# Layer-norm statistics of a Swin block: channels folded to 64 a half, one group of products in place of two, and the deviations spread by way of memory

## The chip, the cores and the metric

The kernel runs on one NeuronCore of a Trainium2 chip. The metric is the device time of one execution in microseconds (us). Each kernel ran several times; a "fast" run is one within 1.5% of the fastest of its kernel. PE is TensorE, PEld its weight loads, DVE is VectorE, ACT is ScalarE, POOL is GpSimd, SP the engine that issues most transfers.

## The reference

The input is 16 images of 192 channels, 56 x 56, fp32. The first layer is a Swin block with shifted 7 x 7 windows, the second a dynamic 3 x 3 depthwise convolution. What matters here are the two layer norms over the 192 channels of every token:

```python
def _ln(x, g, b, eps=1e-05):
    mu = x.mean(-1, keepdims=True)
    var = ((x - mu) ** 2).mean(-1, keepdims=True)
    return (x - mu) / jnp.sqrt(var + eps) * g + b

h = _ln(transpose(x), norm1_g, norm1_b)      # before the attention
...                                          # windows, qkv, softmax, projection
x1 = shortcut + transpose(h)
y = _ln(transpose(x1), norm2_g, norm2_b)     # before the MLP
y = gelu(y @ fc1_w + fc1_b) @ fc2_w + fc2_b
return x1 + transpose(y)                     # the convolution follows
```

## The kernel before

An image is cut into 4 steps. A step holds two halves h of 392 tokens (`T`). Channels lie on partitions: `v0[128, 2, T]` has the first 128 channels of both halves, `v1[128, T]` the other 64, half 0 on partitions 0 to 63 and half 1 on 64 to 127. 64 steps are pipelined: while the MLP of step i-2 and the attention of step i run, "side 0" prepares norm 1 of step i+2 or i+3 (names `1_...`) and "side 1" prepares norm 2 of step i-1 or i (names `2_...`).

The channel sums come from products with a constant `sel` of 1/192. The 192 channels are first folded to 128:

```python
def norm_squares(key, i, side, engine, adder=None, tags=None):
    ...
    if engine is nc.scalar:
        for h in range(2) if tags else (slice(0, 2),):
            nc.scalar.activation(s0[:, h], v0[:, h], AF.Square)
        nc.scalar.activation(s1, v1, AF.Square)
    else:
        engine.tensor_tensor(s0, v0, v0, ALU.mult)
        engine.tensor_tensor(s1, v1, v1, ALU.mult)
    ...     # on GpSimd, for each half: s0[p, h] += s1[p]

def norm_sums(key, i, side):
    ...     # xs: copies of v0, and on GpSimd for each half: xs[p, h] = v0[p, h] + v1[p]

def norm_stats(keys, steps):
    ...
    for k in (0, 2) if folded else range(3):
        for side in keys:
            for h in range(2):
                p = (side if k < 2 else 1 - side) * 64 + h * 32
                dst = stats[side][p : p + 32, :T]
                if k == 0 and folded:
                    mm(dst, sel[:, 0], xss[keys[side]][:, h], True, True)
                ...
                else:
                    mm(dst, sel[:, 0], sqs[keys[side]][:, h], True, True)

def norm_spread(keys, d, queues=(nc.sync,), tags=("dv1", "sq01"), order=(1, 0)):
    ...     # for each side, half and block of 32 partitions: one copy of 32 rows
            queues[...].dma_start(v[p : p + 32, h], d[at : at + 32])
```

The MLP's first product is where the statistics sit. `take(f)` gives product f its PSUM banks A, B, C, D, A, B; `gelu(f)` on ScalarE empties them; `between()` puts the statistics into C:

```python
for f in range(3):
    take(f); long(dsts[f], wf1, cols(f), y0, True)
for f in range(3):
    short(dsts[f], wf1, cols(f), y1, False); gelu(f)
after()                     # ScalarE and VectorE: pieces of the convolution
for f in range(3, NFC):
    take(f); short(dsts[f], wf1, cols(f), y1, True)
between()                   # norm_stats into bank C, norm_vars
for f in range(3, NFC):
    long(dsts[f], wf1, cols(f), y0, False); gelu(f)
```

So the short products 4 and 5 wait for the gelus 0 and 1, and the statistics wait for gelu 2.

Names in the profile: `ph` is this first product of the MLP and `hid` what the gelus make of it, `st` the statistics, `dev` and `dv` the deviations (at last their reciprocals) before and after the spread, `yn` the normalised input of the MLP and `win` that of the attention, `sc` the attention scores and `e` their sums with the biases, `pq`, `pk` and `pe` the queries and keys, `y` a piece of the convolution.

## Time and profile before

| before | value |
|---|---|
| time, median | 3108.94 us (3107.64 to 3109.79, 4 runs) |
| loop step, start of ph to start of ph | mostly 47.0 to 47.1 us, every fourth 47.5 |
| statistics in a loop step | 1.45 to 1.55 us, in two steps 1.59 and 1.62 |
| granted TensorE clock | 0.994 |

In each group of instructions the first number is busy time, the second the mean duration of one, and behind the bar stands the engine's idle time just before, with what ended it. Idle time of an engine that is not the bottleneck costs nothing. The prediction reads the page; one view that it did not use matters later, the waits of the weight loads between 200 and 2950 us (columns: who waited for whom, us in total, times, longest):

```profile
PEld sc L92 <- ACT hid L630: 32.6, 58, 0.8
PEld st L92 <- ACT hid L630: 32.4, 58, 0.6
PEld ph L92 <- ACT hid L630: 13.3, 47, 0.4
```

Weight loads run ahead of the products, so such a wait need not cost TensorE anything: its products waited 0.2 us in the same stretch. But it names what the products are close to waiting for: the gelus (`hid`), for ph, st and the scores.

### The profile page before, as it was taken

Reading aid. Unit: us, or ns where it says so; the run is one execution under the profiler, and the core shown is the slowest. Engines: PE = TensorE matmul, PEld = TensorE weight load, DVE = VectorE, ACT = ScalarE, POOL = GpSimd, SP = SyncE. Lnnn points to the kernel's source line nnn. Section 1 sums busy time; section 2 is a strip of 40 time slices with the busy share of each in tenths; the row PEclk is TensorE's granted clock in tenths of the full one; section 3 lists DMA queues with packets and bytes.
Section 4 is the critical chain, followed back from the end, with each engine's and each line's share of the span. In section 5 each row is a group of like instructions: output and inputs, shape, how many; then the busy total and the mean of one; then the engine's idle time right before and its main releaser. Section 6 shows DMA issues by size and latency. Waiting matters only on the chain.

```text
span 3105.7 us, 64444 instructions
## 1 busy us (share of the span) xinstructions
PE 3073.1 (99%) x25670; PEld 1927.8 (62%) x25670; DVE 2118.6 (68%) x3893; ACT 1880.4 (61%) x2989; POOL 1245.4 (40%) x1165
## 2 busy tenths in 40 slices
PE   8999999999999999999999999999999999999998
PEld 5566666666666666666666666666666666666654
DVE  6665676776776766866866767667667668667664
ACT  4665665665655655656656656556556556566553
POOL 7534434334334334344344343343343343443321
PEclk8999999999999999999999999999999999999999
DMA  4102121121211112121121211212111121211101
GB/s 114 30 19 63 41 70 37 45 67 43 68 43 51 52 51 66 35 71 41 43 69 41 70 38 43 69 43 67 45 45 56 48 71 35 65 46 43 35 30 55
DMA packets 98376, 160.09 MB, mean 52 GB/s; under 512 B 25284, under 2 KB 80556, under 8 KB 96156
## 3 DMA queue, kind: packets, MB, share of 16 engines
q1 hardware_dynamic: 95698, 153.10, 17.7%
q8 instruction: 203, 3.33, 0.5%
q0 software_dynamic: 1872, 2.07, 0.4%
q10 hardware_dynamic: 506, 0.79, 0.1%
q14 instruction: 97, 0.79, 0.1%
HBM read 41.26 MB, written 38.54 MB: 26 GB/s over the span
## 4 chain that ended last, share of the span: by engine, by line
PE 96%; DVE 2%; DMA 1%; ACT 0%; issue 0%; POOL 0%; POOLq 0%; DVEq 0%; ACTq 0%
PE ph L92 25%; PE pf L92 24%; PE pv L92 8%; PE pp L92 8%; PE po L92 6%; PE pq L92 5%; PE pt L540 5%; PE sc L92 4%; PE pk L92 4%; PE pe L92 4%; PE st L92 3%; PE pc L92 0%; DMA rel_r<-in_L_conv_rel_bias_dram 0%; DVE vbd L483 0%; DVE e L518 0%
## 5 line engine op out<-in xcount | busy, mean ns | idle before, releaser
L92 PE MATMUL pf<-hid,wf 128*128 128x392 f32 (+1 forms) x3072 | 802.9, 494 | 3.5 <-ACT hid L630 2.0
L92 PE MATMUL ph<-yn,wf 128*128 128x392 f32 (+1 forms) x3072 | 799.1, 497 | 0.3 <-DVE x L616 0.3
L527 POOL TENSOR_TENSOR prob<-e,tot 113x588 f32<-113x588 f32 x256 | 297.7, 1174 | 1126.3 <-DVE tot L526 1126.1
L92 PEld LDWEIGHTS ph<-yn,wf 128*128 128x128 f32 (+1 forms) x3072 | 426.3, 188 | 344.8 <-issue 77.6
L92 PEld LDWEIGHTS pf<-hid,wf 128*128 128x128 f32 (+1 forms) x3072 | 386.9, 164 | 303.2 <-issue 119.7
L483 ACT COPY vbd<-pv 49x192 f32<-49x192 f32 x512 | 160.1, 313 | 682.8 <-DVE vbd L483 678.3
L676 DVE SCALAR_TENSOR_TENSOR x<-pf,cols,x 128x784 f32<-128x784 f32 (+1 forms) x128 | 106.1, 829 | 530.3 <-PE pf L92 494.8
L630 ACT ACTIVATE hid<-ph,f1b 128x784 f32<-128x784 f32 x384 | 336.8, 913 | 102.3 <-PE ph L92 100.8
L266 POOL TENSOR_TENSOR sq<-sq,sq 64x392 f32<-64x392 f32 x252 | 260.8, 1035 | 261.6 <-ACT sq L257 248.2
L280 POOL TENSOR_TENSOR xs<-x,x 64x392 f32<-64x392 f32 x246 | 249.0, 1012 | 231.8 <-DVE x L616 222.5
L740 DVE SCALAR_TENSOR_TENSOR y<-x,wt,y 128x770 f32<-128x770 f32 x282 | 320.1, 1145 | 16.2 <-ACT y L732 8.8
L92 PEld LDWEIGHTS pv<-wqkv,win 64*128 64x128 f32 (+1 forms) x2048 | 255.5, 189 | 30.8 <-issue 0.7
L92 PE MATMUL pv<-wqkv,win 64*128 64x192 f32 (+1 forms) x2048 | 272.3, 326 | 0.0
L518 DVE TENSOR_TENSOR e<-e,top 113x588 f32<-113x588 f32 x256 | 264.0, 1031 | 8.9
L92 PE MATMUL pp<-o,wp 128*128 128x392 f32 (+2 forms) x896 | 251.4, 514 | 0.0
L546 ACT COPY prt<-pt 128x678 f32<-128x678 f32 x256 | 179.2, 727 | 117.1 <-PE pt L540 115.6
L245 ACT ACT_TABLE_LOAD x192 | 246.3, 1283 | 5.2 <-issue 1.8
L511 DVE TENSOR_TENSOR e<-sc,bias_t 113x588 f32<-113x588 f32 x256 | 179.5, 763 | 96.9 <-PE sc L92 96.8
L521 ACT ACTIVATE e<-e 113x588 f32<-113x588 f32 x256 | 176.8, 691 | 110.4 <-DVE e L518 110.4
L540 PEld LDWEIGHTS pt<-ident,prob 113*128 113x128 f32 x1536 | 165.5, 141 | 65.4 <-issue 36.1
L92 PE MATMUL po<-prt,vbd 128*64 128x49 f32 x6144 | 197.1, 224 | 0.4 <-ACT prt L546 0.4
L92 PEld LDWEIGHTS po<-prt,vbd 128*64 128x64 f32 x6144 | 188.9, 138 | 9.7 <-ACT prt L546 0.6
(169 smaller groups left out, 4079.9 us busy)
## 6 DMA issues: line engine op xcount, KB each, us to landing
dv<-dev SPq DMA_DIRECT2D x1004, 49.0 KB, 2.0
xs<-x SPq DMA_DIRECT2D x246, 98.0 KB, 2.2
x<-in_x_dram SPq DMA_DIRECT2D x15, 1484.0 KB, 6.7
out_dram<-y SPq DMA_DIRECT2D x48, 392.0 KB, 2.4
out_dram<-y SPq DMA_DIRECT2D x48, 196.0 KB, 3.2
x<-in_x_dram SPq DMA_DIRECT2D x16, 392.0 KB, 4.5
x<-in_x_dram SPq DMA_DIRECT2D x15, 350.0 KB, 5.5
out_dram<-y SPq DMA_DIRECT2D x16, 308.0 KB, 2.2
```

What stands on the lines that cost most here:

```text
L92: nc.tensor.matmul(dst, lhs, rhs, start=start, stop=stop, skip_group_check=True)
L245: nc.scalar.activation(junk, eps_t[0:1], func)
L266: adder.tensor_tensor(s0[p, h], s0[p, h], s1[p], ALU.add)
L280: nc.gpsimd.tensor_tensor(s0[p, h], v0[p, h], v1[p], ALU.add)
L511: nc.vector.tensor_tensor(e, sc[:PW, :, : HEADS * N], rel, ALU.add)
L518: nc.vector.tensor_tensor(ehs[wp], ehs[wp], t.broadcast_to([PW, 2 * HEADS, N]), ALU.subtract)
L521: nc.scalar.activation(es[wp], es[wp], AF.Exp)
L527: nc.gpsimd.tensor_tensor(prob[wp][:PW, :, 0:N], ehs[wp], t.broadcast_to([PW, 2 * HEADS, N]), ALU.mult)
L540: nc.tensor.transpose(pt[:, a, g * PW : (g + 1) * PW], prob[wp][:PW, h : h + 2, :].rearrange("p h k -> p (h k)"), ident[:PW, :PW],)
L546: nc.scalar.copy(prt, pt[:, :, : 3 * PW])
L630: nc.scalar.activation(hid[:, f], phs[f][:, :, :T], AF.Gelu, bias=f1b[:, f : f + 1])
L740: nc.vector.scalar_tensor_tensor(dst, src, wt[:, kc, t : t + 1], dst, ALU.mult, ALU.add)
```

## The change

The intent is to halve TensorE's time for the statistics. x and the squares of a half are folded further, from 128 channels to 64, which leaves room for both halves on 128 partitions: half 0 on partitions 0 to 63, half 1 on 64 to 127. One product then gives both halves, and both sides' x and squares fill the four column groups at once. The price is a third addition for x and a second kind of square for the crossed-over copy. The reciprocal deviations then go to memory in one transfer and come back by one broadcast read for each side, 3 transfers in place of 16. At the start, the first spread is made by two products and the first normalisation goes ahead of the biases.

```diff
+    def norm_folded(key, i, side):
+        ...
+        own = [(slice(h * 64, h * 64 + 64), h) for h in range(2)]
+        def copies():
+            nc.sync.dma_start(xs[0:64, 1], v0[64:128, 0])
+            nc.sync.dma_start(xs[64:128, 1], v0[0:64, 1])
+        def sums():
+            for p, h in own:
+                nc.gpsimd.tensor_tensor(xs[p, 0], v0[p, h], v1[p], ALU.add)
+            nc.gpsimd.tensor_tensor(xs[:, 0], xs[:, 0], xs[:, 1], ALU.add)
+        def squares(engine):
+            ...                       # s1 = v1 * v1 on GpSimd (2_) or ScalarE (1_)
+            return [
+                lambda: [nc.scalar.activation(s0[p, 0], v0[p, h], AF.Square) for p, h in own],
+                lambda: nc.scalar.activation(s0[:, 1], xs[:, 1], AF.Square),
+            ]
+        def fold():
+            nc.gpsimd.tensor_tensor(s0[:, 0], s0[:, 0], s1, ALU.add)
+            nc.gpsimd.tensor_tensor(s0[:, 0], s0[:, 0], s0[:, 1], ALU.add)
...
     def norm_stats(keys, steps, st):
+            if folded:
+                streams[side] = [(2, x_)]
+                streams[side + 2] = [(2, q_)]
...
+            mm(st[at * 32 : at * 32 + 32, 0, :T], sel[:, which], src, k == 0, k == n - 1)
...
     def norm_vars(keys, st, tag="dev"):        # was: one Square and one subtract for each side
+        nc.scalar.activation(part, st[lo:hi, 0, :T], AF.Square)
+        nc.vector.tensor_tensor(part, st[64 + lo : 64 + hi, 0, :T], part, ALU.subtract)
...
     def norm_spread(keys, part, tags=("dv1", "sq01"), order=(1, 0)):
+        nc.sync.dma_start(rows, part[::16])
...
+            nc.sync.dma_start(
+                v,
+                rows[at : at + 2].rearrange("(o h) t -> o h t", o=1).broadcast_to([128, 2, T]),
+            )
...                                             # end of a loop step
-            norm_sums(f"2_{i}", i, 1)
+            copies, sums_, squares, fold = norm_folded(f"2_{i}", i, 1)
+            copies()
+            rest = squares(nc.gpsimd)
+            sums_()
...
-            norm_squares(f"2_{i}", i, 1, nc.scalar)
+            for f in rest:
+                f()
+            fold()
```

More of the change, by code (lines that the diff above doesn't have):

```diff
@@ L79, in tile_swin_then_dynamic_conv @@
     psum = ctx.enter_context(tc.tile_pool(name="psum", bufs=1, space=bass.MemoryType.PSUM))
+    dram = ctx.enter_context(tc.tile_pool(name="dram", bufs=2, space=bass.MemoryType.DRAM))
     def banks(name, k):
         return psum.tile([128, 2, 512], F32, tag=f"pair{k}", name=name)
-    singles = [None]
-    def bank(k):
-        return singles[0][:, k]
     def mm(dst, lhs, rhs, start, stop):
@@ L239, in flat_of, with norm_squares @@
         return v0.rearrange("p h r c -> p h (r c)"), v1.rearrange("p r c -> p (r c)")
-    sqs, xss, stats = {}, {}, {}
+    sqs, xss = {}, {}
     def table(func):
         nc.scalar.activation(junk, eps_t[0:1], func)
-    def norm_squares(key, i, side, engine, adder=None, tags=None):
+    def norm_squares(key, i, side, engine, tags=None):
         v0, v1 = flat_of(i)
@@ L260, in norm_squares @@
             engine.tensor_tensor(s1, v1, v1, ALU.mult)
-        sqs[key] = s0
-        def add(adder):
-            for h in range(2):
-                p = slice(h * 64, h * 64 + 64)
-                adder.tensor_tensor(s0[p, h], s0[p, h], s1[p], ALU.add)
-        if adder is False:
-            return add
-        add(adder or nc.gpsimd)
-    def norm_sums(key, i, side):
-        v0, v1 = flat_of(i)
-        s0 = one.tile([128, 2, T], F32, tag=("xs", "o")[side], name=f"xs_{key}")
-        nc.sync.dma_start(s0[64:128, 0], v0[64:128, 0])
-        nc.sync.dma_start(s0[0:64, 1], v0[0:64, 1])
-        for h in range(2):
-            p = slice(h * 64, h * 64 + 64)
-            nc.gpsimd.tensor_tensor(s0[p, h], v0[p, h], v1[p], ALU.add)
-        xss[key] = s0
@@ L283, in norm_stats @@
-    def norm_stats(keys, steps):
-        for side in keys:
-            stats[side] = bank(side)
-        folded = all(k in xss for k in keys.values())
-        for k in (0, 2) if folded else range(3):
-            for side in keys:
-                v0, v1 = flat_of(steps[side])
-                for h in range(2):
-                    p = (side if k < 2 else 1 - side) * 64 + h * 32
-                    dst = stats[side][p : p + 32, :T]
-                    if k == 0 and folded:
-                        mm(dst, sel[:, 0], xss[keys[side]][:, h], True, True)
-                    elif k == 0:
-                        mm(dst, sel[:, 0], v0[:, h], True, False)
-                    elif k == 1:
-                        mm(dst, sel[:, 1 + h], v1, False, True)
-                    else:
-                        mm(dst, sel[:, 0], sqs[keys[side]][:, h], True, True)
-        for side in keys:
-            sqs.pop(keys[side])
-            xss.pop(keys[side], None)
@@ L307, in norm_vars @@
-    def norm_vars(keys, tag="dev"):
-        sides = sorted(keys)
-        d = one.tile([128, T], F32, tag=tag, name=f"dev_{keys[sides[0]]}")
-        mean = {s: slice(s * 64, s * 64 + 64) for s in sides}
-        var = {s: slice(64 - s * 64, 128 - s * 64) for s in sides}
-        for s in sides:
-            nc.scalar.activation(d[var[s]], stats[s][mean[s], :T], AF.Square)
-        for s in sides:
-            nc.vector.tensor_tensor(d[var[s]], stats[s][var[s], :T], d[var[s]], ALU.subtract)
-        stats.clear()
-        return d[0:128] if len(sides) == 2 else d[var[sides[0]]], d
+        sqs[key] = s0, s1
@@ new lines, in norm_folded @@
+    def norm_folded(key, i, side):
+        v0, v1 = flat_of(i)
+        xs = one.tile([128, 2, T], F32, tag=("xs", "o")[side], name=f"xs_{key}")
+        s0 = one.tile([128, 2, T], F32, tag=f"sq0{side}", name=f"sq0_{key}")
+        s1 = one.tile([128, T], F32, tag=f"sq1{side}", name=f"sq1_{key}")
+        own = [(slice(h * 64, h * 64 + 64), h) for h in range(2)]
[7 more added lines that the diff above has]
+        def squares(engine):
+            if engine is nc.gpsimd:
+                nc.gpsimd.tensor_tensor(s1, v1, v1, ALU.mult)
+            else:
+                nc.scalar.activation(s1, v1, AF.Square)
+            return [
[5 more added lines that the diff above has]
+            nc.gpsimd.tensor_tensor(s0[:, 0], s0[:, 0], s0[:, 1], ALU.add)
+        xss[key] = xs[:, 0], s0[:, 0]
+        return copies, sums, squares, fold
@@ new lines, in norm_stats @@
+    def norm_stats(keys, steps, st):
+        folded = all(k in xss for k in keys.values())
+        streams = {}
+        for side, key in keys.items():
+            if folded:
+                x_, q_ = xss.pop(key)
+                streams[side] = [(2, x_)]
+                streams[side + 2] = [(2, q_)]
+            else:
+                v0, v1 = flat_of(steps[side])
+                s0, s1 = sqs.pop(key)
+                streams[side] = [(0, v0[:, 0]), (1, v0[:, 1]), (2, v1)]
+                streams[side + 2] = [(0, s0[:, 0]), (1, s0[:, 1]), (2, s1)]
+        n = 1 if folded else 3
+        order = [(k, at) for k in range(n) for at in range(4) if at in streams]
+        if len(streams) == 2:
+            order.sort(key=lambda o: o[1])
+        for k, at in order:
+            which, src = streams[at][k]
+            mm(st[at * 32 : at * 32 + 32, 0, :T], sel[:, which], src, k == 0, k == n - 1)
@@ L320, in norm_root, with norm_vars, norm_spread @@
+    def norm_vars(keys, st, tag="dev"):
+        lo, hi = min(keys) * 32, max(keys) * 32 + 32
+        d = one.tile([128, T], F32, tag=tag, name=f"dev_{keys[min(keys)]}")
+        part = d[64 + lo : 64 + hi]
+        nc.scalar.activation(part, st[lo:hi, 0, :T], AF.Square)
+        nc.vector.tensor_tensor(part, st[64 + lo : 64 + hi, 0, :T], part, ALU.subtract)
+        return part, d
     def norm_root(part):
         nc.scalar.activation(part, part, AF.Sqrt, bias=eps_t[0 : part.shape[0]])
-    def norm_spread(keys, d, queues=(nc.sync,), tags=("dv1", "sq01"), order=(1, 0)):
+    def norm_spread(keys, part, tags=("dv1", "sq01"), order=(1, 0)):
+        rows = dram.tile([2 * len(keys), T], F32, tag="rows", name=f"rows_{keys[min(keys)]}")
+        nc.sync.dma_start(rows, part[::16])
@@ L329, in norm_spread @@
             v = one.tile([128, 2, T], F32, tag=tags[side], name=f"dv_{keys[side]}")
-            for h in range(2):
-                at = 64 - side * 64 + h * 32
-                for p in range(0, 128, 32):
-                    queues[p // 32 % len(queues)].dma_start(v[p : p + 32, h], d[at : at + 32])
+            at = 2 * (side - min(keys))
+            nc.sync.dma_start(
+                v,
+                rows[at : at + 2].rearrange("(o h) t -> o h t", o=1).broadcast_to([128, 2, T]),
+            )
             out[side] = v
@@ L804, in conv_ready, with stats_of @@
         return ready
-    def stats_of(i):
+    def stats_of(i, st):
         steps = {side: k for side, k in ((0, i + 2), (1, i - 1)) if has(k)}
         keys = {side: f"{side + 1}_{k}" for side, k in steps.items()}
-        norm_stats(keys, steps)
+        norm_stats(keys, steps, st)
         return keys
@@ L815, in tile_swin_then_dynamic_conv @@
     nc.vector.memset(sel, 0.0)
-    nc.vector.memset(sel[:, 0], 1.0 / DIM)
-    nc.vector.memset(sel[0:64, 1], 1.0 / DIM)
-    nc.vector.memset(sel[64:128, 2], 1.0 / DIM)
+    nc.vector.memset(sel[:, 0, 0:16], 1.0 / DIM)
+    nc.vector.memset(sel[:, 1, 16:32], 1.0 / DIM)
+    nc.vector.memset(sel[0:64, 2, 0:16], 1.0 / DIM)
+    nc.vector.memset(sel[64:128, 2, 16:32], 1.0 / DIM)
     nc.vector.memset(ones, 1.0 / DIM)
@@ L883, in tile_swin_then_dynamic_conv @@
     g1, be1, bq, bk, bv = columns(*rows1, 2, nc.vector.tensor_copy)
-    norm_squares("1_0", 0, 0, nc.scalar, nc.vector, ("yn0", "q4"))
+    norm_squares("1_0", 0, 0, nc.scalar, ("yn0", "q4"))
     fold_scale(
@@ L896, in tile_swin_then_dynamic_conv @@
     )
-    singles[0] = banks("st_a", 3)
+    st = banks("st_a", 3)
     keys = {0: "1_0"}
-    norm_stats(keys, {0: 0})
-    part, dev = norm_vars(keys, "o")
+    norm_stats(keys, {0: 0}, st)
+    part, _ = norm_vars(keys, st, "o")
     norm_root(part)
@@ L904, in tile_swin_then_dynamic_conv @@
     norm_squares("1_2", 2, 1, nc.gpsimd)
-    add = norm_squares("1_1", 1, 0, nc.scalar, False)
-    dvs.update(norm_spread(keys, dev, (nc.sync, nc.scalar)))
+    norm_squares("1_1", 1, 0, nc.scalar)
     pm = fold_means(wqkv, 3 * DIM, "fq", 0)
+    pd = banks("dv_0", 3)
+    for h in range(2):
+        pick_row = ident[64:96, 64 + h * 16 : 65 + h * 16].broadcast_to([32, 128])
+        mm(pd[:, h, :T], pick_row, part, True, True)
     fold_center(wqkv, 3 * DIM, pm)
-    add(nc.vector)
     pq = banks("qkb_p", 2)[:, 0]
@@ L920, in tile_swin_then_dynamic_conv @@
         shift(pq[at : at + n, c : c + 1], raw, lo, n, be1)
-    biases(0, 0)
+    norm1_scale(0, pd[:, :, :T], nc.vector)
     for dst, c, at, _, n, b in parts:
@@ L926, in tile_swin_then_dynamic_conv @@
     nc.vector.tensor_scalar(kb, pick, qkb[:, 1:2], None, ALU.mult)
-    norm1_scale(0, dvs.pop(0), nc.vector)
+    biases(0, 0)
     nc.gpsimd.memset(kbd, 0.0)
@@ L932, in tile_swin_then_dynamic_conv @@
         nc.gpsimd.memset(t, 0.0)
-    singles[0] = banks("st_b", 3)
+    st = banks("st_b", 3)
     keys = {0: "1_1", 1: "1_2"}
-    norm_stats(keys, {0: 1, 1: 2})
-    part, dev = norm_vars(keys)
+    norm_stats(keys, {0: 1, 1: 2}, st)
+    part, _ = norm_vars(keys, st)
     norm_root(part)
@@ L942, in tile_swin_then_dynamic_conv @@
     nc.vector.reciprocal(part, part)
-    dvs.update(
-        norm_spread(keys, dev, (nc.sync, nc.gpsimd), tags=("dv1", "yn0"), order=(0, 1))
-    )
+    dvs.update(norm_spread(keys, part, tags=("dv1", "yn0"), order=(0, 1)))
     images[1] = load_x(1, nc.sync)
@@ L1032, in tile_swin_then_dynamic_conv @@
     norm_squares("2_0", 0, 1, nc.scalar)
-    singles[0] = banks("st_c", 3)
+    st = banks("st_c", 3)
     keys = {0: "1_3", 1: "2_0"}
-    norm_stats(keys, {0: 3, 1: 0})
+    norm_stats(keys, {0: 3, 1: 0}, st)
     qs[2], outs = attention_qk(2, 2, 0, 1)
@@ L1041, in tile_swin_then_dynamic_conv @@
     fold_center(wf1, HID, pm)
-    part, dev = norm_vars(keys)
+    part, _ = norm_vars(keys, st)
     table(AF.Sqrt)
@@ L1049, in tile_swin_then_dynamic_conv @@
     nc.vector.reciprocal(part, part)
-    dvs.update(norm_spread(keys, dev, (nc.sync, nc.gpsimd)))
+    dvs.update(norm_spread(keys, part))
     outs[0]()
@@ L1059, in tile_swin_then_dynamic_conv @@
     v_whole()
-    norm_sums("1_4", 4, 0)
+    copies, sums_, squares, fold = norm_folded("1_4", 4, 0)
+    copies()
+    for f in squares(nc.scalar):
+        f()
+    sums_()
     yns[0] = norm2_scale(0, dvs.pop(1), True)
-    norm_squares("1_4", 4, 0, nc.gpsimd)
+    fold()
     attention_v_out(pvs)
@@ L1068, in tile_swin_then_dynamic_conv @@
     residual(1, pp, pair1)
-    norm_sums("2_1", 1, 1)
-    norm_squares("2_1", 1, 1, nc.scalar)
+    copies, sums_, squares, fold = norm_folded("2_1", 1, 1)
+    copies()
+    for f in squares(nc.gpsimd):
+        f()
+    sums_()
+    fold()
     nc.vector.reciprocal(s, s)
@@ L1104, in between @@
         def between():
-            singles[0] = banks(f"st_{i}", C)
-            keys.update(stats_of(i))
+            st = banks(f"st_{i}", C)
+            keys.update(stats_of(i, st))
             if keys:
-                var.append(norm_vars(keys))
+                var.append(norm_vars(keys, st)[0])
             for c, y in zip(cs[1:], ys[1:]):
@@ L1114, in tile_swin_then_dynamic_conv @@
         mlp_first(i - 2, yns.pop(i - 2), hid, (A, B_, C, D, A, B_), after, between)
-        for part, dev in var:
+        for part in var:
             table(AF.Sqrt)
             norm_root(part)
+        if has(i + 3):
+            copies, sums_, squares, fold = norm_folded(f"1_{i + 3}", i + 3, 0)
+            copies()
         outs = [lambda: None] * 4
@@ L1142, in tile_swin_then_dynamic_conv @@
             share(3)
-        for part, dev in var:
+        for part in var:
             nc.vector.reciprocal(part, part)
-            dvs.update(norm_spread(keys, dev))
+            dvs.update(norm_spread(keys, part))
         prts = []
@@ L1159, in tile_swin_then_dynamic_conv @@
         if has(i + 3):
-            norm_sums(f"1_{i + 3}", i + 3, 0)
-            norm_squares(f"1_{i + 3}", i + 3, 0, nc.gpsimd)
+            sums_()
         if 1 in keys:
@@ L1165, in tile_swin_then_dynamic_conv @@
             o = attention_rows(i, attention_values(i, prts, D, C))
+        if has(i + 3):
+            for f in squares(nc.scalar):
+                f()
+            fold()
         pf1 = mlp_narrow(i - 2, hid, A)
@@ L1186, in tile_swin_then_dynamic_conv @@
             residual(i, pp, pair1, at)
-            norm_sums(f"2_{i}", i, 1)
+            copies, sums_, squares, fold = norm_folded(f"2_{i}", i, 1)
+            copies()
+            rest = squares(nc.gpsimd)
+            sums_()
         else:
@@ L1193, in tile_swin_then_dynamic_conv @@
         if has(i):
-            norm_squares(f"2_{i}", i, 1, nc.scalar)
+            for f in rest:
+                f()
+            fold()
         if pt is not None:
```

## The prediction

> **What bounds the kernel now.** I read the page's engine totals first, then the table of busy time by stretch, then the chain that ended last in order of time, and last the timelines of the engines that feed TensorE. From the page, the span and the busy times, and the shares of the chain:
>
> ```profile
> span 3105.7 us, 64444 instructions
> PE 3073.1 (99%) x25670; PEld 1927.8 (62%) x25670; DVE 2118.6 (68%) x3893; ACT 1880.4 (61%) x2989; POOL 1245.4 (40%) x1165
> PE 96%; DVE 2%; DMA 1%; ACT 0%; issue 0%; POOL 0%; POOLq 0%; DVEq 0%; ACTq 0%
> ```
>
> TensorE (PE) is busy 99% of the span and carries 96% of the chain. The busy times by stretch say where the other 1% lies (columns: stretch, its length, then busy us and instructions of PE, weight loads, VectorE, ScalarE and GpSimd, the granted clock, DMA share, GB/s):
>
> ```profile
> 200.00:2990.00 2790.00, 2789.82 (x23563) 1757.09 (x23562) 1935.35 (x3543) 1725.85 (x2744) 1104.56 (x993) 1.00 0.18 51
> 0.00:110.30 110.30, 94.25 (x771) 61.72 (x772) 71.57 (x167) 54.44 (x98) 81.78 (x119) 0.89 0.36 90
> 2988.13:3105.70 117.57, 101.24 (x570) 54.78 (x569) 59.86 (x85) 48.19 (x70) 21.78 (x20) 0.95 0.16 48
> ```
>
> In the loop PE stands still 0.18 us of 2790. The 33 us in which it does stand still are 16 us of prologue and 16 us of the end. So in the loop only PE time counts, and work taken from other engines is worth nothing; the question is whether the work that moves makes PE wait.
>
> The chain in order of time (columns: start, us, what) prices the part that changes, the statistics products, three lines from the loop and two from the last steps:
>
> ```profile
> 1580.75 1.52 PE st L92 x16
> 2808.03 1.53 PE st L92 x16
> 2902.33 1.53 PE st L92 x16
> 2949.87 0.80 PE st L92 x8
> 2996.23 0.84 PE st L92 x8
> ```
>
> A loop step issues 16 records, two per fp32 product: 4 products of folded x, then 4 of folded squares. They take 1.45 to 1.55 us of the chain. The last steps have one side only, so 4 products in 8 records, one to each of the four column groups: 0.80 to 0.84 us. **That is the shape the change gives to every loop step**, so the trace already holds its price.
>
> **What the Trainium skill says.** "TensorEngine Tiling (Array Packing)", section "Tiling Modes": 128x32 gives four tiles that "can execute LdWeights and Matmul in parallel", and changing the mode drains the array. The trace agrees: 8 records of 392 columns in 0.80 us, against 1.32 us for 4 full-width records of pk, and the second group of st begins 0.68 us after the first (1580.68 and 1581.36), so about 0.15 us of the stage is the change of mode and stays.
> "DMA: Bandwidth & Descriptors", section "Anatomy of one DMA": a fixed cost near 2 us, mostly the receipt; its section "Two DMAs through the same engine are not ordered" asks the issuer to wait for the first transfer before a second reads its bytes. Here a 49 KB copy lands in 2.0 us, so the way by memory pays the fixed cost twice.
> "GPSIMD Engine Reference", section "Specifications": SBUF interfaces shared with VectorE, contention with VectorE instructions that have two SBUF inputs. The trace agrees: the subtraction e (two SBUF inputs) takes 0.77 us alone and 1.31 us beside a GpSimd product, while the vbd copies from PSUM take 2.94 us for eight with GpSimd beside them and 2.95 without.
>
> **The change, part by part.**
>
> *Statistics products.* Removed: 4 of 8 products in a loop step. 1.51 us (mean of what I read) to 0.81 us saves 0.70 us. The steps with both sides are i = 2 to 61, 60 steps (492 xs records = 60 x 8 + 3 x 4). **60 x 0.70 = 42 us, all on PE's path.** The three one-sided steps gain nothing.
>
> *ScalarE.* The variance square goes from two of 0.49 us to one, VectorE's subtraction from two of 0.56 to one: off the path. The squares of 1_ move from GpSimd to ScalarE, some 4 x 0.45 us, into its 10.5 us gap before the vbd copies: hidden. The squares of 2_ become three instructions instead of two. This one lies close to the path:
>
> ```profile
> 1575.75 0.86 ACT L256 ACTIVATE sq<-x 128x784 f32<-128x784 f32 x1
> 1576.51 0.51 ACT L257 ACTIVATE sq<-x 128x392 f32<-128x392 f32 x1
> 1576.93 1.02 ACT L732 ACTIVATE y<-x,cols,wt 128x784 f32<-128x784 f32 x1
> 1577.98 2.52 ACT L630 ACTIVATE hid<-ph,f1b 128x784 f32<-128x784 f32 x3
> ```
>
> The three gelus that follow end at 1580.50 and free the banks that the next ph products and st want; st starts at 1580.68. Start to start, the two squares take 1.18 us; three at 0.42 to 0.44 (the pitch of 128x392 here and at the start) take 1.26 to 1.32. So gelu comes 0.1 us later against 0.1 to 0.2 us of slack. I charge 0.05 us a step, 60 x 0.05 = **3 us back**.
>
> *GpSimd.* Before, per step: 4 sums and 4 additions of 64x392 at 1.03 us and squares of 1.49 + 0.84, 10.6 us. After: 6 sums of 1.03, one square of 0.84, 4 additions of 128x392 at about 1.03 (estimate: 64 partitions take that), 11.1 us. Its busy share is 40%. What matters is the 2_ chain at the end of the step: residual, copies (2.0 us to land), third sum, ScalarE's squares, two additions. Now the additions run from 1577.16 to 1579.26, st starts at 1580.68. With the third sum waiting for the copies (about 1574.2) it ends at 1575.3, still before the squares; the additions end at about 1579. No wait. The third sum will run beside VectorE's win products and stretch them by some 0.8 us; VectorE gets 0.56 back and had 0.7 to 2.7 us idle before the scores.
>
> *Spread.* These lines show it in a loop step (SP issuing, GpSimd using):
>
> ```profile
> 1603.11 11.09 SPq L333 DMA_DIRECT2D dv<-dev  x16
> ...
> 1610.93 1.87 POOL L379 TENSOR_TENSOR yn<-x,dv 128x784 f32<-128x784 f32 x1 [2.20 <-DMA dv<-dev]
> ```
>
> From the first issue to the first use 7.8 us pass, 8 issues of 0.69 and 2 us to land. After: one issue and about 2 us to land 6 KB in memory, then a 392 KB read (392 KB of x lands in 4.4 us in a loaded stretch): 0.6 + 2 + 0.6 + 3 to 4.4 = 6.2 to 7.6 us, the other side some 2 us behind, against 13 now. PE wants the normalised rows at 1620.18; by my count the GpSimd work behind them leaves about 4 us. So the spread is **hidden before and after**: worth nothing in the loop.
>
> *Prologue.* The first spread becomes two products on PE, and the biases, which wait for rel_bias until 24.6 us, move behind the first normalisation. VectorE also loses the addition of 3.73 us. pq now starts at 30.87, after win. Then PE's own queue binds: qkb_p ends at 24.4, plus about 1.3 for the two products at the slow clock, plus 4.1 for st_b, gives 29.9: **1 us**, and another 0.5 where the unfolded additions leave st_c. At the end, one spread in the open: GpSimd's half of yn ends at 3055.18 and ph starts at 3055.23, so a slower landing there costs up to 1 us, once.
>
> Sum: 3109 - 42 + 3 - 1.5 + 0.5 = **3069 us**, 1.3% less.
>
> **Rivals.** *The way by memory becomes the bound.* 128 partitions read the same 3 KB at once; no transfer of this trace does that with 392 KB. If one took over 12 us, yn would be late and PE would wait in every step; 3 us a step is 180 us, over 3200. For it: two receipts in series. Against: about 4 us of slack, and idle DMA engines. *The ScalarE or GpSimd chain takes back the gain*: if gelu slips by 0.5 us a step rather than 0.1, 25 us are gone, 3090. For it: the thin slack above. Against: only one short instruction is added. *The start gains more*: rel_bias leaves the path and SP is free 10 us earlier; with all 16 us of the prologue's idle PE gone, 3053. Against: most of those waits (first loads, the vbd copies, the VectorE chain from 70 to 90 us) are untouched.
>
> **Range and chances.** The 42 us are measured in shape, the count is exact; the uncertainty is in small waits (0 to 15 us) and the ends (2 to 6 us better). So 3058 to 3084. Faster by 2% needs 62 us, more than the stage can give with half of it left: 0.03. Slower by 2% needs the spread to fail: 0.03. Within 2%: 0.94.
>
> **What would show it.** Right: st lines of x8 and about 0.81 us in the loop; steps of 46.4 us where 47.1 stand now; PE waiting under 5 us between 200 and 2950; dv reads landing in 3 to 5 us. The ScalarE step is wrong if PE waits for hid before st or ph. The GpSimd step is wrong if PE waits for sq or xs. The spread is wrong if yn waits longer than now and ph waits behind it. The prediction fails as a whole if the one group of four takes clearly over 0.85 us, or if waits of over 0.3 us a step appear.

## The result, and the profile after

The changed kernel took 3080.89 us (median of 4 runs, 3079.76 to 3083.34), the kernel before 3108.94: 28 us or 0.9% less. The ratio is 0.9911, 95% interval 0.9894 to 0.9928, within 2%. A ratio is the mean time of one kernel's fast runs over that of the other's fast runs of the same rounds, so not quite the ratio of the medians.

The sign is as forecast and the time lies in the range, but 12 us of the 40 are missing. The page of the changed kernel (its profiled execution is the slowest of the four, 3083.34 us):

```profile
span 3081.5 us, 62245 instructions
PE 3048.0 (99%) x25182; PEld 1893.6 (61%) x25182; DVE 2116.0 (69%) x3828; ACT 1987.8 (65%) x3230; POOL 1273.1 (41%) x1209
PE 90%; DVE 7%; issue 1%; ACT 0%; DMA 0%; POOL 0%; POOLq 0%; DVEq 0%; ACTq 0%
```

PE is at 99% as before, but its share of the chain has fallen from 96% to 90%, and VectorE has 7%: in places the chain leaves TensorE. The chain in order of time around one loop step (start, us, what), first before:

```profile
1572.65 8.10 PE ph L92 x36
...
1582.27 4.15 PE ph L92 x12
```

and after:

```profile
1561.54 8.39 PE ph L87 x36
1569.93 0.80 PE st L87 x8
1570.72 4.15 PE ph L87 x12
```

The statistics take 0.80 us as forecast (the line of before, 1580.75 1.52, is in the prediction). But the 36 records ahead of them, the same instructions in both kernels, take 8.39 us in place of 8.10. No busy number shows it: from 200 to 2950 us the changed kernel's PE counts as busy for 2748.45 of 2750 us. A record of 392 columns lasts some 0.49 us while the next starts 0.33 us later, so its end covers a short gap. The waits of the weight loads, in the same stretch, do show it:

```profile
PEld ph L87 <- ACT hid L640: 52.5, 114, 0.5
PEld st L87 <- ACT hid L640: 32.4, 58, 0.6
```

Where 47 weight loads of ph waited for a gelu, 114 do now, two in nearly every step. ScalarE's timeline in such a step (start, us, instruction; the step's first ph starts at 1514.72) is to be held against the four lines of the same place in the prediction, whose step starts at 1572.48:

```profile
1516.69 1.29 ACT L493 COPY vbd<-pv 49x192 f32<-49x192 f32 x4 [0.21 <-DVE vbd L493]
1518.00 1.07 ACT L283 ACTIVATE sq<-x 64x392 f32<-64x392 f32 x2
1519.09 0.53 ACT L284 ACTIVATE sq<-xs 128x392 f32<-128x392 f32 x1
1519.53 1.02 ACT L742 ACTIVATE y<-x,cols,wt 128x784 f32<-128x784 f32 x1
1520.58 2.52 ACT L640 ACTIVATE hid<-ph,f1b 128x784 f32<-128x784 f32 x3
```

The squares start 3.28 us into the step (before 3.27), but y starts at 4.81 in place of 4.45: 1.53 us for three squares, not 1.18 for two. The third gelu ends at 8.38 in place of 8.02, and st starts at 8.48 in place of 8.19, 0.11 us after it. So it is from the fifth step to the sixtieth: the gelu ends 0.10 to 0.11 us before st in each, while GpSimd's last addition to the squares was done 0.48 us or more before st (median 1.92). Before, 8.02 + 0.11 = 8.13 lay just under 8.19, where TensorE's own work ends. **The slack was 0.06 us, and the squares come 0.36 later: a wait of 0.30 us.**

Starts of the stages, read from PE's timeline in every step, give the account between the start of the first loop step's ph and the last (2945.0 us before, 2917.8 after):

| summed over 62 steps, us | before | after |
|---|---|---|
| statistics stage | 92.2 | 49.3 |
| first part of ph, over 8.19 a step | 0.3 | 13.7 |
| second part of ph to scores, over 4.145 a step | 0.4 | 2.8 |

That is -42.9 + 13.4 + 2.4 = -27.1, against -27.2 measured. The 13.4 us are 0.29 us in three steps of four and 0.06 in the fourth, where no convolution piece stands between squares and gelu. From here on "the fourth steps" are these, the ones right behind the steps of 47.5 us. The 2.4 us are in the fourth steps only, up to 0.45 each: VectorE's timeline there,

```profile
1613.34 1.76 DVE L365 TENSOR_TENSOR win<-x,dv 128x343 f32<-128x343 f32 x2
1615.02 1.85 DVE L373 TENSOR_TENSOR win<-x,dv 64x343 f32<-64x343 f32 x2
...
1618.07 3.13 DVE L750 SCALAR_TENSOR_TENSOR y<-x,wt,y 128x770 f32<-128x770 f32 x3
1621.23 0.57 DVE L324 TENSOR_TENSOR dev<-st,dev 64x392 f32<-64x392 f32 x1
```

ends its subtraction, which frees the bank of st, at 1621.80, and the scores that want the bank start at 1621.86. That the loop's sum is complete says that the spread brought and cost nothing there.

The start did not gain. pq starts at 31.51 us (before 30.87), and the first loop step at 113.80 (before 110.16). Of the 3.6 us, 2.9 come behind the product pe that starts at 90.29 (before 89.58), and there the granted clock (last but two of the columns) differs; before and after:

```profile
90.00:96.00 6.00, 5.90 (x26) 3.27 (x22) 3.20 (x3) 5.44 (x10) 1.83 (x5) 1.00 0.08 19
```

```profile
90.00:96.00 6.00, 5.71 (x13) 2.80 (x14) 3.31 (x3) 2.44 (x4) 1.98 (x3) 0.50 0.01 4
```

In this execution the clock was at half from 89.5 to 96.3 us, which begins in a wait of 2.6 us for VectorE's weights. All seven traces with the new start have this wait; one more of them (e2) ran at half behind it, for 3.4 us, and five stayed at 1.00. The three with the old start wait 1.0 us there and stayed at 1.00. From the last ph on, the end is 0.7 us shorter.

### The profile page after: what moved, and what is told of

Read it like the earlier page. It is cut to its first block, busy times and chain, and to the rows that moved or that the text cites. A ratio compares the mean times of both kernels' runs of the same rounds, so it can differ in the third digit from the quotient of the medians.

```text
span 3081.5 us, 62245 instructions
## 1 busy us (share of the span) xinstructions
PE 3048.0 (99%) x25182; PEld 1893.6 (61%) x25182; DVE 2116.0 (69%) x3828; ACT 1987.8 (65%) x3230; POOL 1273.1 (41%) x1209
## 3 DMA queue, kind: packets, MB, share of 16 engines
q0 software_dynamic: 1360, 1.26, 0.3%
## 4 chain that ended last, share of the span: by engine, by line
PE 90%; DVE 7%; issue 1%; ACT 0%; DMA 0%; POOL 0%; POOLq 0%; DVEq 0%; ACTq 0%
PE pf L87 24%; PE ph L87 21%; PE pp L87 8%; PE pv L87 7%; PE po L87 6%; PE pq L87 5%; PE pt L550 5%; PE sc L87 4%; PE pk L87 4%; PE pe L87 4%; DVE vbd L493 1%; PE st L87 1%; DVE win L365 1%; DVE win L373 1%; DVE y L750 1%
## 5 line engine op out<-in xcount | busy, mean ns | idle before, releaser
L87 PE MATMUL ph<-yn,wf 128*128 128x392 f32 (+1 forms) x3072 | 812.4, 504 | 0.3 <-DVE x L626 0.3
L87 PEld LDWEIGHTS ph<-yn,wf 128*128 128x128 f32 (+1 forms) x3072 | 418.2, 188 | 366.3 <-issue 76.5
L750 DVE SCALAR_TENSOR_TENSOR y<-x,wt,y 128x770 f32<-128x770 f32 x282 | 286.4, 1025 | 17.3 <-ACT y L742 8.9
L389 POOL TENSOR_TENSOR yn<-x,dv 128x784 f32<-128x784 f32 x62 | 115.6, 1865 | 235.0 <-DMA dv<-rows 235.0
L550 PEld LDWEIGHTS pt<-ident,prob 113*128 113x128 f32 x1536 | 165.5, 141 | 65.4 <-issue 36.1
```

The lines of the kernel that those rows point to most:

```text
L87: nc.tensor.matmul(dst, lhs, rhs, start=start, stop=stop, skip_group_check=True)
L550: nc.tensor.transpose(pt[:, a, g * PW : (g + 1) * PW], prob[wp][:PW, h : h + 2, :].rearrange("p h k -> p (h k)"), ident[:PW, :PW],)
L750: nc.vector.scalar_tensor_tensor(dst, src, wt[:, kc, t : t + 1], dst, ALU.mult, ALU.add)
```

## The experiments

Theory S: the third square on ScalarE, not the wider work on GpSimd or VectorE, took 13 us back. Rival G: GpSimd's longer chain, or the VectorE instructions that it stretches (the prediction's lines: 1.31 us beside a GpSimd product, 0.77 alone), makes TensorE wait. Each run has its own runs of the kernel before on the same chip.

| run | us | ratio to before | ph, three steps of four | ph, fourth |
|---|---|---|---|---|
| changed kernel | 3080.89 | 0.9911 | 8.48 | 8.25 |
| e1_sq_extra | 3110.24 | 1.0002 | 9.05 | 8.82 |
| e2_sq_one (wrong) | 3064.47 | 0.9857 | 8.19 | 8.19 |
| e3_sq_pool1 | 3066.26 | 0.9863 | 8.19 | 8.19 |
| e4_st_half (before, wrong) | 3073.55 | 0.9885 | 8.19 | 8.19 |
| e5_spread_only (before) | 3107.84 | 0.9993 | 8.19 | 8.19 |
| e6_spread_hop | 3081.14 | 0.9907 | 8.48 | 8.25 |
| e7_sq_pool2 | 3071.76 | 0.9877 | 8.19 | 8.19 |
| e8_best | 3064.18 | 0.9852 | 8.19 | 8.19 |

"Before" marks edits of the kernel before, the others are edits of the changed one; "wrong" marks results that are wrong on purpose. The last two columns are the first part of ph, in us from its first start to st's (medians). The interval of each ratio is about 0.0016 to either side; all lie within 2% of 1.

### e1: one square more on ScalarE

```diff
# the loop's 2_ chain; s0x and v0x are its s0[:, 0] and v0
+            nc.scalar.activation(s0x[0:64], v0x[0:64, 0], AF.Square)
             for f in rest:
                 f()
```

> The changed kernel with one of the two 64-partition squares of the end-of-step chain done twice on ScalarE, which adds one instruction of about 0.53 us ahead of the gelus and nothing else. Theory S (the third square on ScalarE delays the gelus that free the banks for the statistics): the slack is already used up, so every loop step with a square waits 0.53 us more, the first part of ph goes from 8.49 to about 9.0 us, 59 steps x 0.53 = 31 us, about 3112 us in all, no faster than the kernel before. Rival G (the longer GpSimd chain and its contention with VectorE make TensorE wait): ScalarE has slack, nothing changes, 3078 to 3084.

Measured: 3110.24 us, 29 more than the changed kernel, and the first part of ph is 9.05 us. The whole gain of the change is gone through one instruction of half a microsecond in each step. The added instruction takes 0.56 us, start to start, and the first part of ph is 0.56 longer in every step with a square: there is no slack left on ScalarE. Here the wait is long enough to show at the products themselves (from one step, whose ph starts at 1526.56):

```profile
1529.84 0.53 ACT L1226 ACTIVATE sq<-x 64x392 f32<-64x392 f32 x1
1533.94 1.73 PE L87 MATMUL ph<-yn,wf 64*128 64x392 f32 x8 [0.44 <-ACT hid L640]
```

### e2: one square less on ScalarE, GpSimd as it is

```diff
-            for f in rest:
-                f()
+            nc.scalar.activation(xss[f"2_{i}"][1], v0x[:, 0], AF.Square)   # 128 partitions at once
+            rest[1]()
```

> The changed kernel with the two 64-partition squares of the end-of-step chain replaced by one of 128 partitions (wrong result on purpose: half the partitions square the wrong half of x). ScalarE is some 0.64 us earlier, GpSimd does exactly the same work. Theory S: the first part of ph returns from 8.49 to 8.19 us in three steps of four, 45 x 0.29 + 14 x 0.06 = 14 us, about 3067 us. Rival G: GpSimd and VectorE do the same as in the changed kernel, so 8.49 stays and the time stays at 3078 to 3084.

Measured: 3064.47 us, ph back at 8.19. GpSimd does the very work of the changed kernel, so rival G falls for the 13 us. The result is wrong by construction, though it passed the tolerance: for channels 64 to 127 of half 1 the squares of half 0's tokens are taken. ScalarE's lines of this run:

```profile
1506.27 0.53 ACT L1225 ACTIVATE sq<-x 128x392 f32<-128x392 f32 x1
1506.70 0.51 ACT L284 ACTIVATE sq<-xs 128x392 f32<-128x392 f32 x1
1507.12 1.02 ACT L742 ACTIVATE y<-x,cols,wt 128x784 f32<-128x784 f32 x1
```

Squares of 128 partitions follow each other at 0.42 to 0.43 us; the two of 64 partitions in the changed kernel took 1.09 us for both. One of them lasts 0.53 us: half the partitions saved nothing and lost the overlap.

### e3: one square moved to GpSimd

```diff
-        def sums():
+        def sums(pool=0):
...
+            for p, h in own[:pool]:
+                nc.gpsimd.tensor_tensor(s0[p, 0], v0[p, h], v0[p, h], ALU.mult)
...
-                lambda: [... AF.Square) for p, h in own],
+                lambda: [... AF.Square) for p, h in own[pool:]],
...
-            rest = squares(nc.gpsimd)
-            sums_()
+            rest = squares(nc.gpsimd, 1)
+            sums_(1)
```

> The changed kernel with one of the two 64-partition squares moved from ScalarE to GpSimd, between the sums: a right result. Theory S: ScalarE is 0.53 us earlier, more than the 0.29 us lost, so the first part of ph is 8.19 us again and the time 3066 to 3072 (the fourth steps, where the scores already wait 0.15 us for VectorE, may lose 0.3 us more, 5 us in all). Rival G: GpSimd has 0.84 us more to do beside VectorE, so it gets slower than the changed kernel, over 3084.

Measured: 3066.26 us, a right result. GpSimd has more to do, TensorE waits less. The step loses its waits for gelu; the fourth steps keep theirs for the scores (4.30 us from the second part of ph to the scores, 2.4 us in all). The waits of the weight loads for gelu in this run have lost the ph line:

```profile
PEld st L87 <- ACT hid L642: 32.4, 58, 0.6
```

### e4: TensorE's part alone

```diff
# kernel before, norm_stats; wrong on purpose: the mean rows get the other side's squares
+        alone = folded and len(keys) == 2
+        if alone:
+            stats[1] = stats[0]
-        for k in (0, 2) if folded else range(3):
+        for k in (2,) if alone else (0, 2) if folded else range(3):
# norm_vars: ALU.add if alone else ALU.subtract, so that the root stays real
```

> The kernel before with the four products of folded x left out of every loop step (wrong result on purpose): TensorE's part of the change alone, no work moved to another engine. Theory: the stage takes 0.80 us in place of 1.51, the first part of ph stays 8.19, 60 x 0.71 = 43 us, about 3066 us: the product alone is worth 43 us and what the changed kernel lacks was given back elsewhere. Rival: the shorter stage itself runs into the gelus or into VectorE behind it and half of the gain is lost, 3080 to 3090.

Measured: 3073.55 us (wrong result, as intended), 35 us less than before, between the two forecasts. The stage takes 0.80 us and the first part of ph 8.19, as the theory says. But in the fourth steps the scores start 4.69 us after the second part of ph, not 4.15: 14 x 0.55 = 7.7 us. There VectorE has two subtractions:

```profile
1612.05 3.13 DVE L744 SCALAR_TENSOR_TENSOR y<-x,wt,y 128x770 f32<-128x770 f32 x3
1615.21 1.14 DVE L320 TENSOR_TENSOR dev<-st,dev 64x392 f32<-64x392 f32 x2
```

So the rival had a part in it: with the stage cut, VectorE's subtraction comes onto the path in the fourth steps. The changed kernel's single subtraction of 0.57 us, which the prediction priced at nothing, spares most of that: its fourth steps lose 2.4 us in sum where these lose 7.7.

### e5: the spread alone

```diff
# kernel before, in the loop
-            dvs.update(norm_spread(keys, dev))
+            dvs.update(norm_spread_mem(keys, dev))   # rows <- d[lo:hi][::32], then a broadcast read a side
```

> The kernel before with only the spread of the loop changed: one transfer of the needed rows to memory and one broadcast read for each side in place of 16 copies. Theory: the spread is hidden before and after, so the time stays, 3105 to 3112 us, the first yn of a step starts some 2 us earlier (the changed kernel shows 10.5 us before the next step against 8.3), and the loop's steps stay at 47.0 to 47.5 us. Rival: the spread by 16 copies loads the transfer engines or GpSimd's queue so that a part of the 28 us comes from here; then 3095 to 3103.

Measured: 3107.84 us, ratio 0.9993 (0.9978 to 1.0008), the loop's steps as before. GpSimd's wait for the deviations ahead of yn falls from 138.7 to 36.1 us in total. Over all loop steps yn starts 10.6 us before the next step (median, 9.3 to 11.4 but for the last), against 8.9 (7.3 to 9.8): 1.7 us earlier, near the 2 us expected. TensorE's time does not change. The spread is hidden either way.

### e6: the spread made longer

```diff
+        hop = dram.tile([2 * len(keys), T], F32, tag="hop", ...)
-        nc.sync.dma_start(rows, part[::16])
+        nc.sync.dma_start(hop, part[::16])
+        nc.sync.dma_start(rows, hop)
```

> The changed kernel with a second trip through memory put into every spread (rows copied from memory to memory before they are read), which makes it some 2 us longer. Theory: hidden behind about 4 us of slack in the loop, 3078 to 3084 us, yn starts some 2 us later and TensorE still waits for nothing there. Rival: the spread is on the edge, each microsecond of it is paid in every step, 60 x 1 to 2 us, over 3130.

Measured: 3081.14 us, as without the hop. GpSimd waits longer before yn, here the changed kernel and then this run:

```profile
1550.83 1.86 POOL L389 TENSOR_TENSOR yn<-x,dv 128x784 f32<-128x784 f32 x1 [3.73 <-DMA dv<-rows]
```

```profile
1550.39 1.86 POOL L391 TENSOR_TENSOR yn<-x,dv 128x784 f32<-128x784 f32 x1 [5.58 <-DMA dv<-rows]
```

1.9 us more in this step, and yn starts 8.7 us before the next ph in place of 10.7 (medians). TensorE pays for it only once, 0.7 us in the last step. The fear that the way by memory might become the bound was unfounded by at least those 2 us.

### e7: both squares moved to GpSimd

The edit is that of e3 with 2 in place of 1.

> Both 64-partition squares moved from ScalarE to GpSimd. Theory S says ScalarE has had its slack back with the first one, so the second brings nothing: 8.19 us in the first part of ph; the fourth steps, where the scores wait for VectorE's subtraction, get up to 0.3 us longer through contention with GpSimd: 3065 to 3072 us, not faster than with one moved. If ScalarE were still the bound it would be some 5 to 10 us faster than with one.

Measured: 3071.76 us, 5.5 more than with one moved. ph stays at 8.19, so ScalarE is no longer the bound; but GpSimd's longer chain now does cost. From the scores to the next step the 61 loop steps are 4.6 us longer in sum than with one square moved. VectorE's `win` products take longer (their durations sum to 321 us from 200 to 2900, in place of 298), and its first addition to the scores starts 1.28 us behind these, not 0.87 (medians). Of the 4.6 us the waits of TensorE show a part, for these additions (the ends of the records cover shorter waits):

```profile
PE pq L87 <- DVE e L523: 2.2, 12, 0.4
```

Near the end, in the step before the last, the squares' group of the statistics waits for GpSimd's last addition, and the stage takes 2.18 us in place of 0.78. The fourth steps' wait for the scores is 0.3 us less. 4.6 + 1.4 - 0.3 = 5.7, all of the difference between the two traces' loops. Rival G is real, but one square further on.

### e8: one square moved, and VectorE's order in the fourth steps

```diff
# on top of e3
-                conv_rest(*c, y, 0 if k else None)
+                conv_rest(*c, y, 0 if k or first else None)
...
-            for c, y in zip(cs[1:], ys[1:]):
+            for c, y in list(zip(cs, ys))[0 if first else 1 :]:
                 conv_rest(*c, y, 1)
```

> One square moved to GpSimd, and in the fourth steps VectorE does its subtraction for the deviations ahead of the last two conv products instead of behind them. Theory: the scores of those steps wait for that subtraction (second part of ph to the scores 4.30 us there against 4.15), so 14 x 0.15 = 2 us less than with the square moved alone, about 3064 us; if the wait is for something else, 4.30 stays and 3066 to 3068.

Measured: 3064.18 us, a right result, ratio 0.9852 to the kernel before: below both kernels, though still within 2% of the kernel before. In the fourth steps the scores now start 4.15 us after the second part of ph. The loop takes 2901.75 us from first to last ph, 43.2 less than before, which is all that the statistics stage had to give. VectorE's order there:

```profile
1604.97 1.02 DVE L752 SCALAR_TENSOR_TENSOR y<-x,wt,y 128x770 f32<-128x770 f32 x1
1606.02 0.57 DVE L326 TENSOR_TENSOR dev<-st,dev 64x392 f32<-64x392 f32 x1
1606.63 2.08 DVE L752 SCALAR_TENSOR_TENSOR y<-x,wt,y 128x770 f32<-128x770 f32 x2
```

## Why the prediction was right, and where it was not

The prediction held: 3069 us in a range of 3058 to 3084, measured 3080.89, and "within 2%" came true. Its mechanism was right. Of the 40 us it forecast, 28 came. The range left 0 to 15 us for small waits; they came to 15.8, and the time lies 3 us below the range's upper end. The terms tell why.

- **Statistics products, "60 x 0.70 = 42 us".** Right: 42.9 us in the loop's account, and e8 has them all, 43.2. The one-sided steps of the trace before were the right place to read the price.
- **ScalarE, "three at 0.42 to 0.44 ... I charge 0.05 us a step ... 3 us back".** This is the step that failed, by size: 13.4 us. Two of its numbers were off. The three squares take 1.53 us, not 1.26 to 1.32, because behind each of the two of 64 partitions the next starts after 0.54 and 0.55 us, and not at the pitch of 128. And the slack was 0.06 us, not 0.1 to 0.2: st cannot start when the gelu ends, it starts 0.11 us later. e1 and e2 show it from both sides. The sign that the prediction named for this step, TensorE waiting for hid before st or ph, showed at the weight loads only.
- **VectorE and GpSimd.** "No wait" for the folded squares was right: the loop's products show no wait for sq or xs. So was the stretching of VectorE's win products by "some 0.8 us": their durations sum to 311 us from 200 to 2900, before to 259, 0.9 a step. That VectorE "gets 0.56 back" off the path was wrong in the fourth steps: the scores wait there for the subtraction, 2.4 us. e8's new order removes that wait, and e4 shows that two subtractions would have cost 7.7.
- **Spread, "worth nothing in the loop".** Right, by e5 and e6. GpSimd does wait longer for the deviations, 214.7 us in place of 125.1 between 200 and 2950, since it comes to yn without the squares that were ahead of it; but yn starts 10.7 us before the next ph, not 8.9 (medians), and ph does not wait for it. The section "Anatomy of one DMA" that the prediction cites has its fixed cost from transfers that GpSimd issues; here SP issues them, and the traces decide: 2.0 us for a copy of 49 KB, 1.7 us from the issue of the 6 KB to that of the reads, and 4.1 us from there to the first use (1546.73 to 1550.83; the page gives no landing times).
- **Prologue, "1 us, and another 0.5".** Not seen. TensorE's queue did bind, but the two spreading products took 2.9 us at the slow clock in each of the seven traces, not 1.3, so pq starts 0.64 us later here and not 1 earlier. Over the traces, the first loop step starts at 110.2 to 112.3 us with the old start (before, e4, e5) and at 108.4 to 113.8 with the new one (the other seven): differences in the first loads and in the clock cover any gain, and the longer wait for VectorE's weights (2.6 us, not 1.0) speaks against one. Whether the new start is worth a microsecond stays open.
- **The end, 0.5 us later.** It is 0.7 us earlier: 49.8 to 50.0 us from the last ph in the eight traces with the spread by memory, e5 and its old start among them, and 50.6 in the two without (before, e4). In the trace before, that ph starts at 3055.16 and GpSimd's yn ends at 3055.18: it followed TensorE's own products and was not held up by yn; the prediction read that place otherwise.
- **"PE waiting under 5 us between 200 and 2950"** was the wrong thing to watch: the trace shows 0.4 us of such waits although 16 us are lost, because the records' ends cover gaps of this size. Steps of 46.65 us in place of the 46.4 forecast, and the waits of the weight loads, show them.

## What to carry to other kernels

When an engine is busy all the time, look for the neighbours that keep it so with no slack, and give their last hundred nanoseconds a number before work is moved to them; the waits of the weight loads list those neighbours even where the products show no wait. Compare the starts of the same stage in every step rather than busy shares. Splitting ScalarE's squares by partitions did not make the parts cheaper here (0.53 us for 64, 0.51 to 0.53 for 128), so of two ways to fold, take the one that adds fewest instructions to the engine that frees the banks.

## What the Trainium skill lacked or had wrong

- "ScalarE: Activation LUTs", section "What ACT_TABLE_LOAD costs", gives 186 ns + 0.833 N for an activation with immediate operands and an overlap of 93 ns between two in a row. For 392 columns that is 0.513 us and a pitch of 0.42, and the squares of 128 partitions agree (0.51 to 0.53 and 0.42 to 0.44 us). It does not say that the overlap can be lost: the two squares of 64 partitions took 1.09 us to the next start. A change from one half to the other is not needed for that: the same 128-partition square starts 0.44 us behind one of 128 partitions (e2), and 0.55 us behind a single one of 64 (e3). Ahead of a square of 64 the overlap stays (0.42 us behind one of 128, in the changed kernel). Why it is lost stays open.
- "TensorE: Matmul & The Clock Gate", section "Why this matters for your kernels", warns of gaps over about 3 us. Here a wait of 2.6 us, 3 us behind one of 0.5, went with a granted clock of 0.50 for 6.8 us in one trace and for 3.4 us in another (e2); five others with the same waits stayed at 1.00.
- "DMA: Bandwidth & Descriptors": no section has a figure for 128 partitions that read the same 3 KB of memory. Two such reads of 392 KB were issued 1.7 us after the 6 KB transfer to memory, and the first was in use 5.8 us after that transfer's issue (1545.03 to 1550.83).
- "TensorEngine Tiling (Array Packing)", section "Tiling Modes", agrees with what was measured: 8 records of a quarter of the columns took 0.80 us, where 8 full-width ones at 0.33 us would take 2.6 (an estimate). It has no number for a change of tiling mode, which would be about 0.15 us of the 0.80 here (an estimate, 0.80 less two rounds of 0.33; no run takes it apart).
